# The last product's result turned to rows by VectorE in squares of 32 and by transfers in runs of 128 bytes, all but two regions

## The chip, the cores and the metric

One NeuronCore of a Trainium2 chip runs the whole kernel in one launch. The time is the device time of an execution in microseconds; beside it stands the span, which the profile measures from the first to the last instruction. In the text PE is TensorE, DVE VectorE, ACT ScalarE, POOL GpSimd and SP SyncE. SP and ACT each issue transfers on a queue of their own (q1 and q10 in the profile); both queues are served by the core's 16 DMA engines.

## The reference

A graph of 3327 nodes with 512 features each, all in float32, goes through two layers. Both use the same adjacency matrix.

```python
# layer 0
h = maximum(layernorm(x), 0)
q, k, v = h @ Wq.T + bq, h @ Wk.T + bk, h @ Wv.T + bv
x = x + softmax(q @ k.T / sqrt(512) + adj + adj) @ v
# layer 1
h = maximum(layernorm(x), 0)
A2 = adj + eye(3327)
dscale = diagonal(A2) ** (-0.5)
temp = A2 @ h @ W.T
x = x + relu((dscale[:, None] * A2 * dscale[None, :]) @ temp)
```

## The kernel before

The rows are padded to 26 tiles of 128 (`NT = 26`). After the scores of layer 0 come three large products of a 3328 x 3328 matrix with a matrix of 512 columns, numbered `g = 0, 1, 2`: the softmax weights times the normalised rows, A2 times the normalised rows of layer 1, and A2 times the scaled `temp`. All three run by a two-level recursion that needs seven products instead of eight at each level. The order of the seven outer products is `ORDER` (line 30: p5, p1, p6, p7, p2, p3, p4).

The columns of the left matrix, which are the rows of the result, lie in two strips `s` with two halves `y` each. A half of strip 0 is seven tiles wide (`H[0] = 896`), one of strip 1 six (`H[1] = 768`). For every outer product and strip there are seven steps: six with a pair of inner tiles, in which PE makes 14 matmuls (seven inner products, two for the strip's operands), and one with the odd tile (`None`) with eight. This gives 3 x 7 x 2 x 7 = 294 steps, which `run(k)` records one by one (line 1238). The steps of the last three outer products of `g = 2` are 252 to 293.

The result is held turned: `cts[s][y][d]` is a tile with 128 of the 512 features on the partitions (`d` is the block of features) and the 896 or 768 rows of that half along the free dimension. PE accumulates in eight PSUM banks; DVE and ACT gather them into these tiles at the end of each outer product (`Gather.first`, `rest` and `settle`, lines 948 to 981), and ACT puts earlier parts into the banks beforehand (`seed`, line 940). A region, that is a half `y` and a pair of feature blocks (`z = d // 2`), is complete at different times: both strips of (y=1, z=1) after p7, (0, 0) after p2, (0, 1) after p3, (1, 0) after p4, the last product.

Step `k` records, in this order: the load of step `k + 3`'s left operands on SP (`Step.load`, lines 820 to 827), the loads that are due (`between` tasks with "load" in their name), the matmuls of step `k`, the stores that became due (`deliver`, line 787: a store is issued on ACT's queue in a later step than the one that made its data), DVE's sums of operands for step `k + 2` (lines 163 to 165), and the other tasks that are due. The order of every engine's instructions is fixed as recorded (`in_order`, line 111). The built program hands eight completion semaphores for transfers around in turn, for SP's and ACT's transfers together: each issue waits until the eighth transfer before it has landed.

The last matter of the kernel is `finish` (line 1112). For each of the 26 row tiles PE turns four 128 x 128 blocks of `cts` into a PSUM bank (`turned`, line 1098, matmul with the identity, line 1102), ACT applies the relu with the factor `sd` of each row while reading the bank (line 1118), DVE adds the row tile of layer 0's result, which `finish_load` (line 1086) brought from `x1d` in DRAM (line 1119), and ACT's queue stores 128 rows to `out` (line 1120). Twenty of the tiles are done whole, one or two in a step, between steps 274 and 291, some of them in the middle of a step's matmuls (`within`). Tiles 20 to 25 (strip 1, y = 1) are done in two halves: the features of z = 1 in steps 254 to 259, those of z = 0 after the last step, by `turn_last` and `finish` from six different banks. `sd` is made at step 6 from the diagonal of the adjacency matrix, loaded in single elements (`prepare`, line 732; `prepared`, line 734).

`by_32` (line 147) holds 104 columns, one for each 32 rows. Before, it serves for the row sums of the softmax alone: DVE turns the sums in squares of 32 (line 596), and `place_totals` at step 3 reads the tile by a matmul (line 666).

## Time and profile before

| | us |
|---|---|
| median of 3 runs | 2166.16 |
| lowest and highest run | 2164.62, 2168.46 |
| the profiled execution | 2166.74 |
| its span | 2164.9 |

The profiled execution took 1.8 us more than its span. Busy shares by fortieths of the span, in tenths (9 is 90% or more), and the DMA queues of the whole run (packets, MB, share of the 16 engines' time):

```profile
PE   9999999999999999999999999999999999999998
PEld 5555555555555555555454555555666655555555
DVE  7479888888888688767777778886666567777676
ACT  5312211112110000001111000010111100001011
POOL 2000000000000000000111000000000000000000
PEclk9999999999999999999999999999999999999999
DMA  8678888888988899889797889886646368766695
...
q1 hardware_dynamic: 263096, 514.97, 70.2%
q10 hardware_dynamic: 35424, 69.62, 8.8%
```

A fortieth is 54 us. The steps 252 to 293 lie in the last four of them, from 1951.4 to 2153.0 us after the span's start. q1 is SP's queue, q10 ACT's. In the windows view each line gives a stretch in us from the span's start, its length, the busy time and number of instructions of PE, PEld (weight loads), DVE, ACT and POOL, the clock that PE was granted, the share of the DMA engines and GB/s.

### The profile page before, as it was taken

To read this page: it belongs to the slowest core of one execution; us is meant where nothing else is said; L and a number is where in the kernel's file an instruction comes from. 1 tells how busy PE (TensorE), PEld (TensorE's weight loads), DVE (VectorE), ACT (ScalarE), POOL (GpSimd) and SP (SyncE) were. 2 spreads that over 40 slices of the span, in tenths; PEclk is the share of its full clock that TensorE was granted. 3 is DMA by queue.
4 is the path that set the end of the run, shared out by engine and by line. 5 is a ranking of instruction groups with operands and counts; after the bars stand their busy time and mean duration, and the time that the engine had idled before them with its cause. 6 is when DMAs were issued, how large, how long until landed. Compare 5 with 4: busy or idle time off the path is not lost.

```text
span 2164.9 us, 21057 instructions
## 1 busy us (share of the span) xinstructions
PE 2148.5 (99%) x6364; PEld 1189.5 (55%) x6364; DVE 1627.2 (75%) x3218; ACT 289.6 (13%) x467; POOL 51.1 (2%) x62
## 2 busy tenths in 40 slices
PE   9999999999999999999999999999999999999998
PEld 5555555555555555555454555555666655555555
DVE  7479888888888688767777778886666567777676
ACT  5312211112110000001111000010111100001011
POOL 2000000000000000000111000000000000000000
PEclk9999999999999999999999999999999999999999
DMA  8678888888988899889797889886646368766695
GB/s 299 214 256 301 295 311 280 305 294 299 334 302 301 292 365 335 279 291 311 264 314 258 301 296 373 300 301 217 207 133 225 129 193 294 245 191 211 211 312 191
DMA packets 298643, 586.02 MB, mean 271 GB/s; under 512 B 31244, under 2 KB 166296, under 8 KB 298520
## 3 DMA queue, kind: packets, MB, share of 16 engines
q1 hardware_dynamic: 263096, 514.97, 70.2%
q10 hardware_dynamic: 35424, 69.62, 8.8%
q8 instruction: 53, 0.87, 0.2%
q14 instruction: 70, 0.57, 0.1%
HBM read 416.63 MB, written 167.84 MB: 270 GB/s over the span
## 4 chain that ended last, share of the span: by engine, by line
PE 92%; DVE 4%; DMA 3%; issue 1%; POOL 0%; ACT 0%; SPq 0%; DVEq 0%; ACTq 0%
PE p L909 54%; PE Y L541 13%; PE Z L541 6%; PE p L900 5%; PE p L1012 4%; PE pw L1073 3%; PE X L541 3%; PE Y L397 2%; DMA rows<-row 1%; PE Z L397 1%; DMA part<-p 1%; PE pt L1102 1%; PE X L397 0%; DVE part L163 0%; DMA wk<-in_wk_dram 0%
## 5 line engine op out<-in xcount | busy, mean ns | idle before, releaser
L909 PE MATMUL p<-part,b 128*128 128x448 f32 (+1 forms) x3528 | 1262.3, 513 | 1.0 <-DVE part L164 0.5
L909 PEld LDWEIGHTS p<-part,b 128*128 128x128 f32 x3528 | 667.6, 190 | 536.1 <-issue 287.7
L163 DVE TENSOR_TENSOR part<-part 128x896 f32<-128x896 f32 (+1 forms) x252 | 256.9, 1019 | 69.8 <-DMA part<-sum 27.9
L541 PE MATMUL Y<-qt,hp 128*128 128x448 f32 (+1 forms) x832 | 308.2, 513 | 1.0 <-DVE g L545 0.6
L541 PEld LDWEIGHTS Y<-qt,hp 128*128 128x128 f32 x832 | 157.7, 190 | 134.7 <-issue 72.7
L541 PE MATMUL Z<-qt,hp 128*128 128x384 f32 (+1 forms) x416 | 162.3, 512 | 0.0
L165 DVE TENSOR_TENSOR part<-part,part 128x448 f32<-128x448 f32 (+1 forms) x219 | 129.5, 591 | 15.3 <-PE p L909 0.5
L164 DVE TENSOR_TENSOR part<-part,part 128x448 f32<-128x448 f32 (+1 forms) x219 | 129.4, 591 | 7.2
L900 PE MATMUL p<-part,b 128*128 128x448 f32 (+1 forms) x336 | 124.2, 513 | 0.0
L541 PEld LDWEIGHTS Z<-qt,hp 128*128 128x128 f32 x416 | 79.0, 190 | 66.2 <-issue 37.9
L545 DVE SCALAR_TENSOR_TENSOR g<-g,Y 128x384 f32<-128x384 f32 (+1 forms) x156 | 91.4, 586 | 29.9 <-PE Y L541 28.8
L900 PEld LDWEIGHTS p<-part,b 128*128 128x128 f32 x336 | 63.7, 190 | 53.5 <-issue 31.4
L952 ACT COPY part<-p 128x384 f32<-128x384 f32 (+1 forms) x33 | 16.6, 502 | 551.2 <-PE p L909 428.4
L548 ACT ACTIVATE g<-g 128x768 f32<-128x768 f32 (+1 forms) x48 | 43.0, 896 | 345.3 <-DVE g L545 303.0
L541 PE MATMUL X<-qt,hp 128*128 128x384 f32 (+1 forms) x208 | 81.1, 512 | 0.0
L953 DVE TENSOR_TENSOR part<-p,part 128x384 f32<-128x384 f32 (+1 forms) x33 | 19.3, 585 | 68.1 <-PE p L909 65.0
L1012 PE MATMUL p<-w,ct 128*128 128x512 f32 x136 | 61.6, 592 | 0.0
L541 PEld LDWEIGHTS X<-qt,hp 128*128 128x128 f32 x208 | 39.5, 190 | 33.1 <-issue 19.3
L972 DVE TENSOR_TENSOR ct<-p,part 128x448 f32<-128x448 f32 (+1 forms) x72 | 43.0, 611 | 19.4 <-PE p L900 14.4
L1073 PE MATMUL pw<-w,rows 128*128 128x256 f32 x208 | 53.5, 380 | 0.4 <-DVE rows L1063 0.4
L1003 DVE TENSOR_TENSOR job<-job 128x896 f32<-128x896 f32 (+1 forms) x52 | 52.9, 1018 | 0.1
L190 POOL TENSOR_TENSOR rstd<-ve,mhalf 128x1 f32<-128x1 f32 x46 | 38.3, 835 | 556.5 <-DVE ve L188 520.8
(191 smaller groups left out, 1679.7 us busy)
## 6 DMA issues: line engine op xcount, KB each, us to landing
part<-sum SPq DMA_DIRECT2D x104, 448.0 KB, 4.9
part<-p SPq DMA_DIRECT2D x91, 448.0 KB, 5.8
part<-sum SPq DMA_DIRECT2D x104, 384.0 KB, 3.6
part<-p SPq DMA_DIRECT2D x91, 384.0 KB, 4.1
part<-in_adjT_dram SPq DMA_DIRECT2D x78, 448.0 KB, 5.0
b<-row SPq DMA_DIRECT2D x234, 128.0 KB, 4.7
part<-in_adjT_dram SPq DMA_DIRECT2D x78, 384.0 KB, 3.7
g<-in_adjT_dram SPq DMA_DIRECT2D x52, 448.0 KB, 4.1
```

What stands on the lines that cost most here:

```text
L163: yield nc.vector.tensor_add(o[:, 0:2], g[:, 0:4:3], g[:, 1:2].to_broadcast([P, 2, g.shape[-1]]))
L164: yield nc.vector.tensor_add(o[:, 2], o[:, 1], g[:, 0])
L165: yield nc.vector.tensor_add(o[:, 3], o[:, 2], g[:, 2])
L397: nc.tensor.matmul(ps[:, :w], M[B[name]][:, c, o * P : (o + 1) * P], hp[k][:, A[name], c], start=start and c == 0, stop=c == 1, skip_group ...
L541: nc.tensor.matmul(ps[:, :wd], h_of(self.t, name, k), qt[B[name]][:, k], start=start and k == 0, stop=k == 1, skip_group_check=True)
L545: nc.vector.scalar_tensor_tensor(a[n], a[n], 2.0, ps[:, :wd], op0=ALU.mult, op1=ALU.add if sign > 0 else ALU.subtract)
L548: nc.scalar.activation(g[1], g[1], AF.Exp, **({"bias": pad} if self.t == HALF - 1 else {}))
L900: yield nc.tensor.matmul(ps[("p2", "p3", "p4", "p8")[k]][:, :w], b[:, z], a[:, 0, y], start=k == 3 and not self.seeded, stop=True, skip_gr ...
L909: yield nc.tensor.matmul(ps[r][:, :w], b[:, i], m, start=self.t == 0 and not adds, stop=self.t == PAIRS - 1 and r in ("p1", "p5", "p6", "p ...
L1003: nc.vector.tensor_add(self.a, self.a, self.b)
L1012: nc.tensor.matmul(ps, cts[s][y][d][:, k * P : (k + 1) * P], w[d], start=d == 0, stop=d == DC - 1)
L1073: nc.tensor.matmul(ps, a, W[B[name]][:, c], start=new and c == 0, stop=c == 1, skip_group_check=True)
```

## The change

The unit of the turning is no longer a row tile but a column block `Columns(s, y, d)`: the whole tile `cts[s][y][d]`, 128 features by 896 or 768 rows. Of the 16 blocks 14 are turned without PE, eight of strip 0 and six of strip 1. What is left to the old way are the last two, d = 0 and 1 of strip 1, y = 1, that is the first half of the features of row tiles 20 to 25, after the last step.

A column block is loaded, turned, scaled and added in four tasks:

- `load`, two steps ahead: the matching part of layer 0's result is read from DRAM by four transfers on ACT's queue, one for each 32 partitions. Partition 32a + r of the tile receives, for each j, the 32 numbers of row 32j + r at features 128d + 32a onward, a run of 128 bytes; a transfer has 32 x 28 or 32 x 24 such runs.
- `turn`: one DVE instruction turns all squares of 32 x 32 of the tile. Partition 32a + r then holds the same runs, of the result, as the loaded tile does.
- `scale`, one step later: relu and the factor of each row in one DVE instruction. The factors come from `by_32`, which now also holds `(diagonal + 1) ** -0.5`, in each group of 32 partitions anew; each is read 32 times in a row.
- `add`, one more step later: DVE adds the loaded tile, and four stores in runs of 128 bytes are posted to ACT's queue.

The blocks begin at step 252 and follow each other every three steps, the last two steps after the one before. Two tiles take turns for the loaded part and two for the turned one. For the factors, four transfers on SP's queue at step 5 load the diagonal into `by_32`, once for each 32 partitions, 3,328 single elements each; at step 11 DVE adds one and POOL takes the power. `x1d` becomes one DRAM tensor for each strip and half instead of one for each row tile. `sd` stays for the tiles of the old way and for `temp`.

```diff
-    x1d = [dram.tile([P, D], F32, name=f"x1d{i}") for i in range(NT)]
+    x1d = [[dram.tile([HT[s] * P, D], F32, name=f"x1d{s}{y}") for y in range(2)] for s in range(2)]
...
+    def load_diagonal():
+        with nc.allow_non_contiguous_dma(reason="the diagonal, once"):
+            for a in range(4):
+                nc.sync.dma_start(by_32[32 * a : 32 * a + 32], bass.AP(tensor=adjT.tensor, offset=adjT.offset,
+                                                                      ap=[[LD + 1, 32], [32 * (LD + 1), 4 * NT]]))
+
+    def scales():
+        nc.vector.tensor_scalar(by_32, by_32, 1.0, None, op0=ALU.add)
+        nc.gpsimd.tensor_tensor(by_32, by_32, mhalf.to_broadcast(by_32.shape), op=ALU.pow)
...
+    xp_slots = itertools.cycle([lambda k=k: view(2, 1)[:, 2 * k : 2 * k + 2].rearrange("p a w -> p (a w)") for k in range(2)])
+    turn_ring = ring(*spare[:2])
...
-    def finish_load(i, z=(0, 1)):
-        c0, c1 = z[0] * E, (z[-1] + 1) * E
-        xrs[i] = next(xr_slots)()
-        nc.scalar.dma_start(xrs[i][:, c0:c1], x1d[i][:, c0:c1])
...
+    class Columns:
+
+
+        def __init__(self, s, y, d):
+            self.s, self.y, self.d = s, y, d
+
+        def parts(self, tile, rows):
+
+            rows = rows.rearrange("(j r) (c a e) -> c a r j e", r=32, a=4, e=32)
+            return [(tile[32 * a : 32 * a + 32].rearrange("r (j e) -> r j e", e=32), rows[self.d, a]) for a in range(4)]
+
+        def load(self):
+            self.x = next(xp_slots)()[:, : H[self.s]]
+            for to, rows in self.parts(self.x, x1d[self.s][self.y]):
+                nc.scalar.dma_start(to, rows)
+
+        def turn(self):
+            self.o = turn_ring([P, H[0]], "turned")[:, : H[self.s]]
+            nc.vector.transpose(self.o, cts[self.s][self.y][self.d])
+
+        def scale(self):
+            j = (STRIPS[self.s] + self.y * HT[self.s]) * 4
+            o = self.o.rearrange("p (j e) -> p j e", e=32)
+            by = by_32[:, j : j + 4 * HT[self.s]].unsqueeze(2).to_broadcast(o.shape)
+            nc.vector.scalar_tensor_tensor(o, o, 0.0, by, op0=ALU.max, op1=ALU.mult)
+
+        def add(self):
+            nc.vector.tensor_add(self.o, self.o, self.x)
+            r0 = (STRIPS[self.s] + self.y * HT[self.s]) * P
+            for of, rows in self.parts(self.o, out[r0 : r0 + H[self.s]]):
+                post(rows, of)
...
-    within = {}
-    for (n, s, t), its in {
-        (5, 1, 1): (0,), (5, 1, 2): (1,), (5, 1, 3): (2,), (5, 1, 4): (3,), (5, 1, 5): (4,),
-        (6, 0, 1): (5,), (6, 0, 2): (6, 14), (6, 0, 3): (15, 16), (6, 0, 4): (17, 18),
-        (6, 1, 1): (19, 7), (6, 1, 2): (8, 9), (6, 1, 3): (10, 11), (6, 1, 4): (12, 13),
-    }.items():
...
-    for t, i in enumerate(range(20, NT)):
-        rows(2, number_of(2, 4, 0, t + 2), i, (1,))
+    k = number_of(2, 4, 0, 0)
+    for n, (s, y, d) in enumerate(((0, 1, 2), (0, 1, 3), (1, 1, 2), (1, 1, 3), (0, 0, 0), (0, 0, 1), (1, 0, 0),
+                                   (1, 0, 1), (0, 0, 2), (0, 0, 3), (1, 0, 2), (1, 0, 3), (0, 1, 0), (0, 1, 1))):
+        part = Columns(s, y, d)
+        for what, later in ((part.load, -2), (part.turn, 0), (part.scale, 1), (part.add, 2)):
+            at(k + later, what)
+        k += 3 if n < 12 else 2
...
-    for k, what in ((1, totals), (3, place_totals), (2, prepare), (6, prepared), (8, judge), (9, judged)):
+    for k, what in ((1, totals), (3, place_totals), (2, prepare), (6, prepared), (5, load_diagonal), (11, scales), (8, judge), (9, judged)):
```

## The prediction

> **What bounds the kernel now.** First the page's busy table and the chain of waits. The chain runs through TensorE (PE) for 92% of the span, PE is busy for 99% of it at the full granted clock; so the time is the sum of PE's instructions, as long as their operands are there in time.
>
> ```profile
> PE 2148.5 (99%) x6364; PEld 1189.5 (55%) x6364; DVE 1627.2 (75%) x3218; ACT 289.6 (13%) x467; POOL 51.1 (2%) x62
> ...
> PE 92%; DVE 4%; DMA 3%; issue 1%; POOL 0%; ACT 0%; SPq 0%; DVEq 0%; ACTq 0%
> ```
>
> Then the stretch that the change touches: the last three recursion products of the third matrix product, steps 252 to 293. In the windows view (busy us of PE, PEld, DVE, ACT, POOL, then clock, DMA share, GB/s) the last line is that stretch, the others its two heaviest parts.
>
> ```profile
> 2051.40:2083.50 32.10, 32.10 (x114) 19.59 (x113) 20.74 (x36) 5.15 (x9) 0.00 (x0) 1.00 0.91 313
> 2083.50:2122.10 38.60, 38.23 (x123) 20.31 (x122) 33.41 (x68) 7.37 (x12) 0.00 (x0) 1.00 0.87 294
> ...
> 1951.40:2153.00 201.60, 201.22 (x640) 112.55 (x639) 142.41 (x268) 29.05 (x51) 0.00 (x0) 1.00 0.72 240
> ```
>
> PE never waits there (0.4 us in 201.6), even where the DMA engines are 91% busy. VectorE (DVE) has 71% of the stretch, the DMA engines 72%. These two resources receive the new work.
>
> **What goes from PE.** Of 104 transposes 92 go: four for each of 20 row tiles, two for each of six. Their cost is the distance between the matmuls around them, in PE's timeline:
>
> ```profile
> 1967.43 0.38 PE L1102 MATMUL pt<-ident,part 128*128 128x128 f32 x2
> 1967.65 5.43 PE L909 MATMUL p<-part,b 128*128 128x448 f32 x14
> ...
> 2065.78 0.60 PE L1102 MATMUL pt<-ident,ct 128*128 128x128 f32 x4
> 2066.22 4.68 PE L909 MATMUL p<-part,b 128*128 128x384 f32 x14
> ```
>
> Four hold up the next matmul by 0.44 us (2065.78 to 2066.22), two by 0.22. 20 x 0.44 + 6 x 0.22 = 10.1 us, all on PE's path: the whole possible gain. The stretch would shrink to 191.5 us. ACT loses its 26 scalings by relu, which delayed nobody but the additions behind them.
>
> **What DVE gets.** 26 additions go (18.39 us for 32, less 2.25 for the six that stay: 16.1). For each of 14 column blocks come a transpose in squares of 32, a relu with scaling by a broadcast factor, and an addition, eight blocks 896 wide, six 768 wide.
>
> ```profile
> 2153.00:2165.00 12.00, 2.25 (x6) 0.78 0.22 72
> sum 213.60, DVE 18.39; mean DVE 2.63
> ...
> L596 DVE STREAM_TRANSPOSE acc<-acc x8: 567/604/639, 245.7 to 631.9; 128x384 f32<-128x384 f32 x4, 128x448 f32<-128x448 f32 x4
> ...
> L163 DVE TENSOR_TENSOR part<-part 128x896 f32<-128x896 f32 x126 | 136.9, 1087 | 47.9 <-DMA part<-sum 22.1 <-DMA part<-p 21.2 <-DMA part<-in_adjT_dram 2.1
> L163 DVE TENSOR_TENSOR part<-part 128x768 f32<-128x768 f32 x126 | 120.0, 952 | 22.0 <-PE p L909 10.2 <-DMA part<-sum 5.8 <-DMA part<-p 3.6
> ```
>
> A transpose of half the width takes up to 0.57 to 0.64 us, so twice that at most, 1.25 and 1.13. The addition is L163's 1.09 and 0.95. The scaling with a broadcast factor has no row; from below it costs the addition (same elements, two sources), from above twice that if the broadcast is slow; I take the addition. 8 x (1.25 + 1.09 + 1.09) + 6 x (1.13 + 0.95 + 0.95) = 45.6 us. DVE then has 142.4 - 16.1 + 45.6 = 171.9 of 191.5 us, 90%. In the tightest part (2083.5 to 2122.1) it has 33.4 - 5.3 = 28.1 us, plus seven new instructions of about 1.03 = 35.3, beside 35.1 of PE (38.6 less eight tiles). That is level; DVE makes its sums two steps ahead (some 10 us), and that lead hides it. If the lead is gone, each microsecond over is one for PE. I allow 1.5 us for this and for product ends; bounds 0 and 5.
>
> **What the DMA engines get.** Each column block is loaded and stored in runs of 32 numbers: 128 x 28 or 128 x 24 packets each way, 8 x 3584 + 6 x 3072 = 47,104, so 94,208 in all. They replace 5,120 packets of 2 KB and 1,536 of 1 KB. Single packets of the trace, by size:
>
> ```
> bytes      4   512  1024  1536  1792  2048  3072  3584
> count  31116    12 39808 49920 45312 42368 44928 44928
> median ns  9  27.5    46    65    74    84   121   140
> ```
>
> This is a straight line, 8 ns plus 0.0371 ns a byte, and the line gives 12.8 ns for 128 bytes. The nearest rows bound it: 9 ns (4 bytes, though mostly single completions; the 3,328 diagonal elements took the same) and 27.5 ns (512 bytes). I take 12.8, near the 4-byte row by size. At these medians the data packets of the stretch now need 122 us of all 16 engines (145 as measured, stretched by contention). The removed ones are 31, the new ones 94,208 x 12.8 / 16 = 75: 166 of 191.5 us, 87%. With 9 ns it is 144, with 27.5 ns 253. Above 17.1 ns the engines no longer get through. Now 91% passes without PE waiting.
>
> [...]
>
> **Queues and waits.** All 112 new transfers are issued from ACT's queue, where 52 stood (0.33 us of issue each: 20 us more on an engine that has over 160 free). All transfers of SP and ACT share eight completion semaphores in turn, so each issue waits for the eighth before it; the profile shows SP held by ACT's transfers:
>
> ```profile
> SPq L847 <- DMA out_dram<-r: 1.6, 3, 1.0
> ...
> SPq L827 <- DMA part<-x1d: 0.9, 1, 0.9
> ...
> q1 hardware_dynamic: 15400, 35.49, 53.6%
> q10 hardware_dynamic: 8352, 12.85, 18.0%
> ...
> dg<-in_adjT_dram SPq DMA_DIRECT2D x1, 13.0 KB, 7.4
> ```
>
> Issues rise from 162 in 201.6 us to some 222 in 191.5, 1.16 per us: eight semaphores then allow a mean landing of 6.9 us, and the stretch's loads and stores now land in 2.6 to 7.3. From 2051.4 to 2083.5 there are already 37 issues in 32.1 us, 1.15 per us, with no PE wait. Behind a blocked store on ACT stand the copy (L952) and the seeds (L946) at each product's end, and behind those DVE's gathering and PE's next banks. I put this at 0 in the forecast; price if the cover is gone below.
>
> **The early part.** Four loads of 3,328 elements bring the diagonal into place at step 5: at 9 ns 7.5 us of all engines, on SP's queue ahead of the next operands (the present load of 3,328 lands in 7.4 us). DVE gets one small addition, POOL a power over 104 columns, four times L737's 5.1 us, while POOL idles. Operands are loaded three steps (some 15 us) ahead, so 0; up to 7.5 if that lead were spent.
>
> **Sum.** The profiled execution took 2166.74 us (span 2164.9 plus 1.8), 0.6 above the median of the runs, 2166.16. 2166.7 - 10.1 + 1.5 = 2158.1; against the median 2157.6. I say 2158.
>
> **Rivals.**
> 1. *The DMA engines become the bound* (slower). A 128-byte packet, above all one written to HBM, costs more than the line says. From 17.1 ns each further ns is 94,208 / 16 = 5.9 us. At 20 ns: 208 of 191.5, so 17 more, 2166.7 - 10.1 + 17 = 2174; at 27.5 ns 61 more, 2218. For it: no row of such stores, 5,900 runs per engine. Against: the straight line from 4 to 3584 bytes. 0.31.
> 2. *ACT's queue becomes the wait.* Column loads stand between PE's bank copies and seeds, waiting for semaphores that slow transfers hold. At six product ends, one landing of 4 to 5 us late, half of it hidden: 6 x 2 = 12 us; 2169, between 2163 and 2175. Against: the same issue rate now costs nothing. 0.13.
> 3. *DVE becomes the bound*: the broadcast scaling at twice the price adds 14 us, 186 of 191.5 with local excess of some 8: 2166, between 2161 and 2172. Against: scaling by a per-partition factor costs what an addition does. 0.09.
> That the transposes stay on PE is ruled out: the built program has 92 fewer.
>
> **How the numbers follow.** Forecast case 0.47, its own range 2154 to 2162. This kernel's measurement tells 0.2%, 4.3 us, from no change. The second rival falls half in no change and half in slower, the third two thirds and one third: faster 0.47, same 0.12, slower 0.41. The range begins at 2154 (the whole 10.1 without allowance, less the runs' spread of 2 us) and reaches to 2195, the first rival at 23.7 ns; beyond lies about a third of that rival, 0.1, and what falls under 2154 or beside the cases, 0.06.
>
> **What would show it.** Right: PE has 92 transposes fewer and still no idle time over 1 us in the stretch; 128-byte packets take near 13 ns; DMA share about 0.9; DVE 0.9. Wrong: PE waits for DVE's sums, and those for operand loads that land after 10 us or more (first rival); copies and seeds on ACT that wait for transfers (second); DVE without gaps while PE waits (third).

## The result, and the profile after

| | us |
|---|---|
| before, median of 6 runs | 2166.74 (2164.62 to 2168.46) |
| after, median of 6 runs | 2186.91 (2185.22 to 2189.25) |
| ratio | 1.0094, 95% interval 1.0081 to 1.0107 |
| the profiled execution after, and its span | 2186.69, 2184.8 |

The change makes the kernel slower, by 20.2 us. The span grows by 19.9 us, so the trace holds the whole loss. In the changed kernel 9 is added to the old line numbers of the matmuls and of the gathering: L909 is now L918 (L900 for the odd step is L909), the seeds are L955, ACT's bank copy L961. New are the column loads (L1141), turns (L1145), scalings (L1151), additions (L1154) and, through the common `post`, the column stores (L795).

The page of the changed kernel, busy table and chain of waits, as before:

```profile
PE 2145.7 (98%) x6272; PEld 1183.8 (54%) x6272; DVE 1653.1 (76%) x3235; ACT 273.0 (12%) x441; POOL 69.1 (3%) x63
...
PE 90%; DMA 4%; DVE 3%; ACTq 1%; issue 1%; ACT 0%; SPq 0%; POOL 0%; DVEq 0%
```

92 instructions and 2.8 us of busy time are gone from PE, and yet it carries 90% of the chain instead of 92%: transfers now end what is followed back. Where PE stands still is seen in its timeline (start, length, count, and in brackets the idle time before it and what ended it), lines of the last stretch:

```profile
1951.60 31.73 PE L918 MATMUL p<-part,b 128*128 128x448 f32 x84
...
2022.67 1.65 PE L909 MATMUL p<-part,b 128*128 128x384 f32 x2 [7.01 <-ACT p L955]
2024.11 33.33 PE L918 MATMUL p<-part,b 128*128 128x448 f32 x84
...
2097.35 1.65 PE L909 MATMUL p<-part,b 128*128 128x384 f32 x2 [7.40 <-ACT p L955]
2098.79 4.22 PE L918 MATMUL p<-part,b 128*128 128x448 f32 x6
2109.19 31.28 PE L918 MATMUL p<-part,b 128*128 128x448 f32 x78 [6.18 <-ACT p L955]
...
2173.22 2.16 PE L1110 MATMUL pt<-ident,part 128*128 128x128 f32 x12
```

The first and the last of these groups in the kernel before:

```profile
1951.65 15.95 PE L909 MATMUL p<-part,b 128*128 128x448 f32 x42
...
2155.14 1.58 PE L1102 MATMUL pt<-ident,part 128*128 128x128 f32 x12
```

Three times PE waits for ACT to put a seed into a bank, at the ends of two products' seven steps of strip 1: once before two matmuls of the odd step of p2, and in p3 there and again a step later. With one short wait of 0.20 that is 20.8 us. ACT's timeline around the first of them says what ACT was doing. `ACTq` lines are transfers being issued; their length is from the first issue of the group to the end of the last:

```profile
2004.84 9.54 ACTq L1141 DMA_DIRECT2D part<-x1d  x4
2016.30 5.28 ACTq L795 DMA_DIRECT2D out_dram<-turned  x4
2021.62 0.48 ACT L961 COPY part<-p 128x384 f32<-128x384 f32 x1 [32.54 <-DMA out_dram<-turned]
2022.13 0.49 ACT L955 ACTIVATE p<-ct 128x384 f32<-128x384 f32 x1
```

Eight issues take from 2004.8 to 2021.6 us, where eight of the old ones needed 8 x 0.34 us (the row stores' line of the kernel before: shortest, median and longest issue in ns):

```profile
L1120 ACTq DMA_DIRECT2D out_dram<-r x26: 338/344/446, 1969.6 to 2149.7; - x26
```

The copy stands behind them in the program, the seed behind the copy, and PE's next two matmuls behind the seed. The copy starts when the last store of a column block has been issued, not when its own bank is ready.

The idle time is not all. In the windows view the granted clock (the third number from the end) after two of the stalls, and well after the first:

```profile
2022.60:2026.10 3.50, 3.43 (x5) 1.85 (x6) 3.33 (x9) 0.02 (x1) 0.00 (x0) 0.50 1.04 145
...
2029.60:2060.30 30.70, 30.70 (x84) 15.46 (x83) 23.41 (x43) 1.08 (x2) 0.00 (x0) 1.00 0.83 202
...
2097.30:2100.80 3.50, 3.45 (x5) 1.85 (x6) 3.29 (x10) 0.00 (x0) 0.00 (x0) 0.50 0.27 38
```

PE comes back at half its clock, 0.50 in both windows. Now the account nearly closes: PE's last transposes start at 2155.1 us before and at 2173.2 after, 18.1 later. Idle time gives +20.4 (20.8, less 0.4 that PE waited before), the transposes that went -10.1, and the lower clock 6.8, which the last section works out from the lines above; 1.0 us of the 18.1 stays open. From there to the end of the span the tail grew from 9.8 to 11.6 us; ACT's last relus also wait for column stores, 8.8 us. 18.1 + 1.8 = 19.9.

What was not it: step 252 began on PE at 1951.60 us after and at 1951.65 before, so no cost of the work in the early part is seen. (In the kernels below with the same early part it began between 1948.8 and 1955.7 us, so a cost of a few us would not show.) And the short packets have the price that was forecast: 87,040 of them between 1951 and 2170 us took 13 ns (median; mean 13.8).

### The profile page after: what moved, and what is told of

Read it like the earlier page. It is cut to its first block, busy times and chain, and to the rows that moved or that the text cites. A ratio compares the mean times of both kernels' runs of the same rounds, so it can differ in the third digit from the quotient of the medians.

```text
span 2184.8 us, 20926 instructions
## 1 busy us (share of the span) xinstructions
PE 2145.7 (98%) x6272; PEld 1183.8 (54%) x6272; DVE 1653.1 (76%) x3235; ACT 273.0 (12%) x441; POOL 69.1 (3%) x63
## 4 chain that ended last, share of the span: by engine, by line
PE 90%; DMA 4%; DVE 3%; ACTq 1%; issue 1%; ACT 0%; SPq 0%; POOL 0%; DVEq 0%
PE p L918 52%; PE Y L541 13%; PE Z L541 7%; PE p L909 4%; PE p L1025 4%; PE pw L1086 3%; PE X L541 3%; PE Y L397 2%; PE Z L397 1%; DMA part<-sum 1%; DMA part<-x1d 1%; DMA part<-in_adjT_dram 1%; ACTq L795 1%; DMA rows<-row 0%; PE X L397 0%
## 5 line engine op out<-in xcount | busy, mean ns | idle before, releaser
L918 PE MATMUL p<-part,b 128*128 128x448 f32 (+1 forms) x3528 | 1263.7, 514 | 7.5 <-ACT p L955 7.0
L918 PEld LDWEIGHTS p<-part,b 128*128 128x128 f32 x3528 | 672.1, 191 | 553.8 <-issue 296.8
L909 PE MATMUL p<-part,b 128*128 128x448 f32 (+1 forms) x336 | 126.2, 518 | 14.4 <-ACT p L955 14.4
L909 PEld LDWEIGHTS p<-part,b 128*128 128x128 f32 x336 | 64.1, 191 | 69.2 <-issue 31.7
L961 ACT COPY part<-p 128x384 f32<-128x384 f32 (+1 forms) x33 | 16.6, 502 | 678.9 <-PE p L918 384.1
```

The costliest lines, as they stand in the source:

```text
L909: yield nc.tensor.matmul(ps[("p2", "p3", "p4", "p8")[k]][:, :w], b[:, z], a[:, 0, y], start=k == 3 and not self.seeded, stop=True, skip_gr ...
L918: yield nc.tensor.matmul(ps[r][:, :w], b[:, i], m, start=self.t == 0 and not adds, stop=self.t == PAIRS - 1 and r in ("p1", "p5", "p6", "p ...
```

## The experiments

Theory Q puts the loss down to ACT's queue: transfers that wait there for completion semaphores hold up copies and seeds. Theory D puts it down to the time and place that the short packets take on the DMA engines. All times are medians, each compared with the kernel before on the same chip (medians of 2166.2 to 2167.7 us); "waits" is PE's idle time over 0.1 us between step 252 and the last transposes, from each kernel's timeline; "landing" is the median time from issue to landing of the column loads and stores between 1985 and 2140 us. Waits and landings belong to the one profiled execution, which can lie some us from the median (e1 2158.4, e7 2175.2, e10 2183.7 us).

| kernel | us | ratio to before (95%) | waits, us | landing, us |
|---|---|---|---|---|
| changed | 2186.9 | 1.0081 to 1.0107 | 20.8 | 5.5, 4.9 |
| e1: columns issued by POOL | 2162.3 | 0.9969 to 0.9988 | 0 | 7.5, 5.5 |
| e2: long runs on ACT | 2163.3 | 0.9971 to 0.9996 | 4.1 | stores 3.7 |
| e3: no column transfers | 2155.2 | 0.9939 to 0.9973 | 0 | - |
| e4: columns issued by SP | 2182.0 | 1.0052 to 1.0085 | 12.5 | - |
| e5: behind copies and seeds | 2186.3 | 1.0067 to 1.0110 | 21.2 | - |
| e6: POOL but for last stores | 2160.3 | 0.9956 to 0.9978 | 1.5 | - |
| e7: loads by POOL | 2178.1 | 1.0033 to 1.0071 | 13.8 | stores 7.7 |
| e8: stores by POOL | 2169.4 | 0.9999 to 1.0018 | 6.8 | loads 5.8 |
| e9: right operands by POOL | 2187.4 | 1.0074 to 1.0105 | 23.4 | 5.3, 4.3 |
| e10: long loads | 2178.9 | 1.0039 to 1.0070 | 14.8 | - |
| e11: long stores | 2173.9 | 1.0025 to 1.0055 | 11.8 | - |
| e12: x1 written turned | 2158.7 | 0.9955 to 0.9979 | 0 | - |
| e13: copies and seeds on DVE | 2185.7 | 1.0063 to 1.0100 | 19.9 | - |
| e14: light operands | 2170.0 | 1.0004 to 1.0023 | 9.1 | 3.6, 3.1 |
| e15: left operands by POOL | 2180.5 | 1.0042 to 1.0075 | 15.2 | 4.8, 4.9 |
| e16: light, and by POOL | 2165.9 | 0.9981 to 1.0000 | 5.2 | 3.7, 3.1 |

**Queue or packets: four extremes.** The first changes the issuing queue alone:

```diff
             for to, rows in self.parts(self.x, x1d[self.s][self.y]):
-                nc.scalar.dma_start(to, rows)
+                nc.gpsimd.dma_start(to, rows)
...
             for of, rows in self.parts(self.o, out[r0 : r0 + H[self.s]]):
-                post(rows, of)
+                posted.append((now[0], lambda of=of, rows=rows: nc.gpsimd.dma_start(rows, of)))
```

> The changed kernel with the column blocks' loads and stores issued by POOL instead of ACT; packets and bytes are the same. Theory Q (ACT's in-order queue: the bank copy and the seeds stand behind column transfers that wait for completion semaphores): PE's 20.8 us of waits for ACT's seeds in the last stretch go, and with them the slower clock after them; about 2157 to 2163 us. Theory D (the DMA engines' time for 128-byte packets is what makes everything late): the engines have the same work, so still 2178 us or more.

The second keeps ACT's queue and the number of transfers, and makes every run as long as a partition of the tile:

```diff
-            for to, rows in self.parts(self.x, x1d[self.s][self.y]):
-                nc.scalar.dma_start(to, rows)
+            for a in range(4):
+                nc.scalar.dma_start(self.x[32 * a : 32 * a + 32], self.flat(x1d[self.s][self.y], a))
```

and the stores likewise.

> As many column transfers on ACT's queue, with the same bytes, but each partition's part in one run of 3584 or 3072 bytes instead of 28 or 24 runs of 128; the numbers land in other places of the result than the reference has them. Theory Q: the number of transfers and the semaphores that they hold are the same, so most of the loss stays, 2175 us or more, and PE still waits for ACT's seeds. Theory D: the 75 us of DMA time for 128-byte packets becomes about 55, the engines are no longer crowded, and the time falls to 2157 to 2163 us.

The third takes the column transfers out; the addition reads the tile that is not turned:

```diff
-            nc.vector.tensor_add(self.o, self.o, self.x)
+            nc.vector.tensor_add(self.o, self.o, cts[self.s][self.y][self.d])
```

> The column blocks are turned, scaled and added on DVE as in the changed kernel, but nothing of them is loaded or stored: the addition takes the unturned tile as its second operand, and 14 of the 16 blocks of the result are not written. Theories Q and D both expect 2156 to 2159 us (the time before less the 10.1 us of transposes, plus little). If DVE's added work is the bound (a third theory), PE waits for DVE's sums and the time stays above 2163 us.

The fourth is the first with `nc.sync` in the place of `nc.gpsimd`.

> The column blocks' loads and stores issued by SP instead of ACT, on the queue of the operand loads. Theory Q in its narrow form (what matters is what stands behind the column transfers on ACT): ACT's copies and seeds are on time, 2157 to 2165 us. If the shared completion semaphores alone are at fault, operands become late instead, PE waits for DVE's sums, and the time is 2170 us or more. Theory D: 2178 us or more.

Either change by itself, another queue (2162.3) or longer runs (2163.3), takes back some 24 us. So neither the queue nor the packets cost alone; the loss needs both. (By the packet prices of the prediction the long runs need 30 us of all engines, not the 55 of the expectation.) Without column transfers the kernel takes 2155.2 us. From the start of step 252 to PE's last transposes it is 193.0 us there (1952.25 to 2145.21) against 203.5 before (1951.65 to 2155.14): 10.5 us less, the 10.1 of the forecast and the 0.4 that PE waited before. The windows view of this kernel:

```profile
1951.40:2150.00 198.60, 195.72 (x568) 106.45 (x566) 172.03 (x296) 15.23 (x32) 0.00 (x0) 1.00 0.57 187
```

DVE is busy for 172.0 us there, and PE never waits for it: DVE is not the bound. On SP's queue the column transfers hold up the operand loads instead (DVE's sums wait 41 us for them); PE then waits mostly for DVE's gathering, 9.3 of 12.5 us, and little is won. On POOL's queue they land later than on ACT's (7.5 and 5.5 us), and PE does not wait: nothing that it needs stands behind them there, and in the built program POOL's transfers count on eight semaphores of their own. So a late landing by itself cost nothing here; nor did the load of the engines as a whole, whose share from 1951.4 to 2150 us is 0.89 here and 0.90 in the changed kernel. POOL's queue shows 3,584 packets of 2 to 4 KB beside completions, where 94,208 runs of 128 bytes are moved: many runs go into one packet. So this experiment changes the packets too, and does not say which of the two helped.

**Is it the order in ACT's queue?** The same transfers on the same queue, but those that are due in the last two steps of a half are recorded behind that half's copy and seeds:

```diff
+        held = 252 <= k < len(steps) - 1 and t in (PAIRS - 1, None)
...
-        deliver(k)
+        if not held:
+            deliver(k)
         if t is None:
...
+        if held and t is None:
+            deliver(k)
+            while later:
+                later.pop(0)()
```

> The changed kernel with the same transfers, in the same runs of 128 bytes, on the same queue (ACT's). Only their place in ACT's program changes: those column loads and stores that the changed kernel issues in the last two steps of a half are issued behind that half's copy and seeds instead of ahead of them. Theory Q (transfers that wait for a completion semaphore hold up the copy and the seeds behind them in ACT's queue): PE's three waits for ACT's seeds, 20.8 us together, go or shrink under 5 us in all, and the time falls by 18 us or more, to 2157 to 2168 us. Theory D (the engines' time for 94,208 short packets is what costs, wherever they stand): 2180 us or more, with waits of PE that now end at DVE's sums or at operand loads. A mixed result of 2168 to 2180 would say that the queue carries some of it and late operand loads the rest.

2186.3 us: nothing won, against the expectation of theory Q; theory D missed as well, as PE's three waits still end at ACT's seeds. ACT's timeline of this kernel:

```profile
1997.05 9.41 ACTq L1141 DMA_DIRECT2D part<-x1d  x4
2007.64 7.62 ACTq L795 DMA_DIRECT2D out_dram<-turned  x4
2015.56 5.42 ACTq L1141 DMA_DIRECT2D part<-x1d  x4
2021.03 0.48 ACT L961 COPY part<-p 128x384 f32<-128x384 f32 x1 [33.32 <-DMA part<-x1d]
```

The copy now has four column transfers fewer ahead of it (32 instead of 36 since the first), and is as late: those that remain have become late in their turn. We read this as ACT running behind by a whole block, so that what stands last in the line does not matter.

**Moving a part to POOL.** Three kernels, each the first one with one thing less: the stores of the last two blocks back on ACT; only the loads on POOL; only the stores on POOL.

> All column transfers issued by POOL as in the first experiment, but for the stores of the last two column blocks, which go back to ACT's queue. In the first experiment PE ended its work 10.7 us earlier than in the kernel before, and the span only 8.4 us earlier: 12.0 us lay between the start of PE's last group and the end, against 9.8 before. If the last stores issued by POOL make this tail (they land later than others and share the engines with the last row stores), the tail falls to 9 to 10.5 us and the time to 2157 to 2160.5 us. If the tail has another cause (contention, whichever queue issues them), the time stays at 2161 to 2164 us; and if the ACT queue's eight stores hold up ACT's last relus as in the changed kernel (8.8 us of wait there), it rises to 2164 us or more.

> Half of the move: the column loads are issued by POOL, the column stores stay on ACT's queue. Theory Q: the copy and the seeds of two of the three stalls stand behind a store and a load in turn; with the loads gone 56 of the 112 transfers still stand in ACT's queue, but the issues that share eight semaphores fall from some 222 to some 166 in the stretch, as many as before the change, so each is had sooner: PE's waits fall from 20.8 to 0 to 6 us and the time to 2160 to 2170 us. Theory D (packets): 2180 to 2190 us, as many short packets run.

> The other half: the column stores are issued by POOL, the column loads stay on ACT's queue. Theory Q: as with the loads moved, 0 to 8 us of PE's waits stay, 2160 to 2172 us; if it is the stores alone that matter (the waits of the copy are put down to a column store each time), this kernel does as well as the one that moves both, 2158 to 2163 us, and the one that moves the loads does worse. Theory D: 2180 to 2190 us; a weaker form of it, that short writes to HBM are what costs, would leave this one at 2180 us or more as well, since the number of short writes is the same.

With the last stores back on ACT the time is 2160.3, and the interval overlaps that of the first kernel. The time is the one expected, but not for the reason expected: the tail after the start of PE's last group is 11.6 us (2147.90 to 2159.5) and not 9 to 10.5. Why this tail is longer than without column transfers (8.7) stays open. Halves give halves: 13.8 us of waits stay with the stores on ACT, 6.8 with the loads. The stores weigh more than the loads, but neither is all of it. For the loads alone both theories missed: 2178.1 us lies above the 2170 of theory Q and below the 2180 of theory D.

**Half of the short packets.** The long runs of the second experiment for the loads alone, then for the stores alone.

> The same 112 transfers on ACT's queue and the same bytes, but the loads in long runs (3.5 and 3 KB), the stores in runs of 128 bytes: half of the short packets. The loaded block is not the one that belongs there, so the sums of 14 blocks are of other numbers. With all short: 2186.9 us and 20.8 us of waits; with none: 2163.3 us and 4.1 us. If each short packet counts alike (the engines' load), this lies half way, 2172 to 2178 us. If short writes to HBM are what lasts, it stays at 2180 to 2187 us; if short reads are, it falls to 2163 to 2170 us.

> The mirror image: the stores in long runs, the loads in runs of 128 bytes; the result of 14 blocks is written to other places. If each short packet counts alike, 2172 to 2178 us; if short writes to HBM are what lasts, 2163 to 2170 us; if short reads are, 2180 to 2187 us.

2178.9 and 2173.9 us: 8.0 and 13.0 of the 23.6 us that both together bring (2186.9 to 2163.3). Short reads and short writes both count; that the writes count more is not clear of the noise, as the two intervals overlap. That short writes to HBM alone are what lasts is ruled out.

**The shared semaphores.** The right operands of the last three products leave SP's queue for POOL's:

```diff
-                nc.sync.dma_start(dst[:, k], src if z is None else src[:, z * E : (z + 1) * E])
+                queue = nc.gpsimd if self.g == 2 and self.r in ("p2", "p3", "p4") else nc.sync
+                queue.dma_start(dst[:, k], src if z is None else src[:, z * E : (z + 1) * E])
```

> The column transfers stay as in the changed kernel: 112 of them, in runs of 128 bytes, on ACT's queue. Instead SyncE is relieved: the right operands' rows of the last three products (p2, p3, p4 of the third matrix product) are loaded by POOL's queue, which has its own semaphores, so about a quarter of the issues that share eight semaphores leave the ring in the stretch, while the DMA engines move the same bytes in the same packets. If what holds ACT back is the common ring of semaphores, in which an ACT transfer waits for one of SyncE's that itself waits for PE, PE's 20.8 us of waits fall to 0 to 8 us and the time to 2160 to 2172 us. If the short packets themselves hold up ACT (each transfer simply takes too long), PE's waits stay at 15 us or more and the time at 2179 us or more.

2187.4 us and 23.4 us of waits: no gain. The mere number of issues that share the semaphores is not what counts.

**Is ACT's queue the link at all?** All transfers stay, and DVE makes the copies and seeds of the last three products:

```diff
-                        nc.scalar.mul(ps[k][:, : self.width], c, sign)
+                        if now[0] >= 252:
+                            nc.vector.tensor_scalar(ps[k][:, : self.width], c, float(sign), None, op0=ALU.mult)
+                        else:
+                            nc.scalar.mul(ps[k][:, : self.width], c, sign)
...
+            if behind:
+                nc.vector.tensor_copy(c11, p["p1"])
+                behind()
```

> The changed kernel with every transfer left as it is (112 column transfers in runs of 128 bytes, on ACT's queue, in the same places). Only the copies and the seeds of the last three recursion products (5 copies and 21 seeds, about 0.5 us each) are made by VectorE instead of ACT, so that no computing that PE waits for stands in ACT's queue behind a transfer. If ACT's in-order queue is the link (theory Q), PE no longer waits for ACT, DVE gains some 13 us of work (185 of some 191 us, so waits of 1 to 3 us for DVE at the ends of halves are to be expected), and the time falls from 2186.9 to 2160 to 2172 us. If the slow transfers reach PE in another way (late operands, late sums, late column blocks that stop DVE), PE's waits stay above 12 us in all, now put down to DVE or to a transfer, and the time stays at 2177 us or more.

2185.7 us, 19.9 us of waits: theory Q as it stood, with ACT's order as the only link, falls. Nothing that PE needs stands behind a transfer on ACT here, and PE waits as long, now for DVE. DVE's timeline tells why:

```profile
2051.60 0.98 DVE L1152 STREAM_TRANSPOSE turned<-ct 128x768 f32<-128x768 f32 x1 [8.46 <-DMA out_dram<-turned]
2083.09 0.96 DVE L1161 TENSOR_TENSOR turned<-turned,part 128x768 f32<-128x768 f32 x1 [9.48 <-DMA part<-x1d]
2091.07 1.11 DVE L1152 STREAM_TRANSPOSE turned<-ct 128x896 f32<-128x896 f32 x1 [4.90 <-DMA out_dram<-turned]
```

Within some 40 us a turn waits 8.5 us for the store that frees its tile, an addition 9.5 us for its load. The column transfers themselves get through too slowly: with two tiles for the loaded part and two for the turned one, a block's loads and stores are not done when the next but one needs the tile. In all DVE waits 37.5 us for column transfers here, and it carries ACT's copies and seeds besides, so the like size of the loss says little. In the changed kernel DVE never waits for them: ACT pays for that lateness and hands it on through its own program (DVE waits 34 us for ACT's copies there); here DVE does. More than two tiles of each kind were not tried. So the question becomes why the transfers are slow.

**Why slow: the company.** The queues view of the changed kernel in two windows of 3 us, first 2014 to 2017, where SP's transfers run too, then 2022 to 2025, where they don't (packets, MB, share of the engines' time, and one load issued in the first window with its time to landing):

```profile
q1 hardware_dynamic: 270, 0.75, 89.1%
q10 hardware_dynamic: 799, 0.10, 21.7%
...
part<-x1d ACTq DMA_DIRECT2D x1, 112.0 KB, 7.2
```

```profile
q10 hardware_dynamic: 3204, 0.40, 85.9%
```

Alone, 1,068 short packets a us pass: 85.9% of 16 engines, 13 ns each. Beside SP's packets of 1 to 3.5 KB it is 266, though a load that was issued at 2014.0 us is under way through the whole window and lands 7.2 us after its issue. Most of the 799 pass at once: 551 in the first half microsecond, and between 2015 and 2017 us only 115, beside 198 of SP's. At these rates the 896 packets of a transfer need 0.8 us in the one case and 3.4 in the other. The price of a packet is the same, a median of 13 ns in both windows; fewer of them get through: beside long packets the queue of short ones got 0.10 MB of 0.85. In what order the engines serve the two queues was not shown; both shares of the first window add up to 111%, so the engines had no time left in it.

The next kernel cuts the company: SP loads the left operands of the last three products for 32 partitions only, in the same packets.

```diff
-            nc.sync.dma_start(a[:, k], adjT[r0 : r0 + P, c0 : c0 + H[s]])
+            nc.sync.dma_start(a[:some, k], adjT[r0 : r0 + some, c0 : c0 + H[s]])
```

> The changed kernel, but the left operands of the last three recursion products are loaded for 32 of 128 partitions only (same packets, a quarter as many; the other 96 partitions keep what stood there, so these products are of other numbers). The number of transfers, their order, the queues and semaphores, and all 94,208 packets of 128 bytes stay. If competition with long packets is what makes the column transfers late, they land in 2 to 4 us, no issue of ACT lasts over 1 us, PE's waits fall from 20.8 us to 0 to 4 us and the time to 2155 to 2164 us. If ACT's queue itself, or the eight semaphores by the number of issues, is what is too slow, the waits stay above 12 us and the time at 2176 us or more.

2170.0 us: between the two expectations, 16.9 us of the 31.7 that lie between the changed kernel and the one without column transfers. The stores' line and their time to landing, from the view by source line; changed kernel first (shortest, median and longest issue in ns, the landing in us):

```profile
L795 ACTq DMA_DIRECT2D out_dram<-turned x40: 322/518/3755, 1984.8 to 2135.1; - x40
...
DMA to landing us min/median/max: 2.0/4.9/7.5
```

```profile
L795 ACTq DMA_DIRECT2D out_dram<-turned x43: 322/539/1008, 1985.5 to 2139.9; - x43
...
DMA to landing us min/median/max: 2.0/3.1/5.1
```

With less company a store lands in 3.1 us instead of 4.9, and no store's issue lasts over 1.0 us, where one lasted 3.8. (The longest issue of a load is 1.9 us, above the 1 us expected, and 2.7 in the changed kernel.) That is a second way in which ACT is held: not only the wait for a semaphore, but the issue of a transfer of many short packets itself becomes long when those before it have not drained; the last section has the counts. With long runs (e2) the longest issue of a store is 0.59 us.

**And the left operands' semaphores.** In what is left in that kernel, the fourth load of a block waits 4.8 us, until 2011.80, for a semaphore. By the order in which the eight are handed around, a left-operand load of SP's holds it, and for 2.7 us of the 4.8 that load has not been issued, as it waits for a matmul to free its tile. POOL takes these loads; with all operand bytes, and with a quarter of them:

```diff
+        queue = nc.gpsimd if late else nc.sync
...
-                nc.sync.dma_start(a[:, k], sumd[s][j][:, SUMS.index(what), :])
+                queue.dma_start(a[:, k], sumd[s][j][:, SUMS.index(what), :])
```

> The changed kernel, but the left operands of the last three recursion products (the loads that wait for PE to free their buffer) are issued by POOL, whose transfers don't take the eight semaphores that SyncE and ACT share. Bytes, short packets, and all of ACT's queue stay. If the waits for semaphores held by such loads are the smaller part and the competition of packets the larger, PE's waits fall from 20.8 to some 8 to 14 us and the time to 2168 to 2180 us. If the shared semaphores are the whole cause after all, to 0 to 3 us and 2155 to 2164 us; if they are nothing, the time stays at 2182 us or more.

> Both at once: the left operands of the last three products issued by POOL, and loaded for 32 of 128 partitions only (these products are of other numbers). If competition and the semaphores held by PE-bound loads are together the whole cause, PE has no wait over 1.5 us left and the time is 2155 to 2162 us, as without any column transfer (2155.2). If 2165 us or more, ACT's queue has a limit of its own for transfers of 768 and 896 packets.

| us (waits of PE) | left operands on SP | on POOL |
|---|---|---|
| all operand bytes | 2186.9 (20.8) | 2180.5 (15.2) |
| a quarter of them | 2170.0 (9.1) | 2165.9 (5.2) |

The two causes add up: the company of long packets 15 to 17 us, the left operands' place among the shared semaphores 4 to 6 us (with all bytes the time is just above the 2180 us that was expected at most). Of the last kernel's expectation the first case, no wait left, was missed: 10.7 us to the 2155.2 without column transfers stay, 5.2 of them waits for ACT. Its other case, 2165 us or more and a limit of ACT's queue of its own, is met by a hair. The 10.7 us can come from the short transfers' own crowd on ACT's queue, or from the right operands and the quarter of the left ones that still run beside them; this was not taken further apart.

**ACT's queue, counted.** In the changed kernel's trace, between 1985 and 2140 us, ACT stands 55 us until the transfer that holds the semaphore of its next issue has landed (4 us in the kernel before), and its 77 issues take another 55 us (16 us for 41 before). Of the 55 us at semaphores, 27 are held by column transfers, 20 by left operands and 7 by right ones, which fits that moving the right ones won nothing; and in only 4 of the 20 had the left operand not yet been issued, so it is mostly the landing that ACT waits for, and less the load's own wait for PE. Both sums together go with PE's waits in the nine kernels that have loads and stores on ACT's queue and its copies too: 85 to 90 us where PE waits 4 to 5 us (e16, e2), 94 to 100 where it waits 9 to 15 (e11, e14, e15), 106 to 128 where it waits 15 to 23 (e5, e9, e10 and the changed kernel).

**A better version.** If x1 is already turned when it is written, in the first matrix product, each column block is loaded by one transfer of long runs. The 104 stores of x1 that this needs, and the column stores, are issued by POOL; what the old way still reads of x1 is stored in rows besides. Nothing of the computation is left out.

```diff
-        post(x1_of(i), xt)
+        s, y, k = where(i)
+        for n in range(4):
+            to = x1t[s][y].rearrange("d (a r) (j e) -> j r (d a) e", r=32, e=32)[4 * k + n]
+            of = xt[32 * n : 32 * n + 32].rearrange("r (c e) -> r c e", e=32)
+            posted.append((now[0], lambda to=to, of=of: nc.gpsimd.dma_start(to, of)))
...
-            for to, rows in self.parts(self.x, x1d[self.s][self.y]):
-                nc.scalar.dma_start(to, rows)
+            nc.scalar.dma_start(self.x, x1t[self.s][self.y][self.d])
```

> A version meant to be better: x1 is written already turned, in the first matrix product (each row tile by four transfers in runs of 128 bytes, issued by POOL), so that a column block is loaded in one transfer of long runs on ACT's queue (14 instead of 56), and the column stores are issued by POOL. All of the computation is done. If ACT's queue and the eight semaphores are what costs, the last stretch has no wait of PE over 1 us, as with both on POOL, and with half as many short packets there its transfers land sooner: 2156 to 2161 us, against 2162.3 with all column transfers on POOL and 2155.2 without any. If the 104 stores of x1 hurt the first matrix product (POOL's queue or short packets there), some of it is given back there: 2162 to 2170 us, with the stretch before step 168 longer than in the kernel before.

2158.7 us in six runs (2157.2 to 2159.6), 0.33% faster than before (interval 0.21% to 0.45%), and as fast as the forecast for the change itself. PE has no wait in the last stretch. The window that was shown for the kernel without column transfers:

```profile
1951.40:2150.00 198.60, 193.43 (x561) 105.23 (x559) 170.21 (x293) 13.88 (x29) 40.77 (x56) 0.99 0.76 242
```

The clock is at 0.99, the DMA share at 0.76 instead of 0.90 in the same window, and the first product gives nothing back: step 252 begins at 1949.95 us, 1.7 earlier than before, which is within the spread given above. From there to PE's last transposes it is 193.0 us, as without column transfers; the tail behind them is longer, 12.6 us instead of 9.8.

## Why the prediction failed, point by point

**PE: right.** 92 transposes are worth 10.1 us; the kernel without column transfers needs 10.5 us less for PE's stretch, and 0.4 of that is a wait that PE had before. That this was the whole possible gain on PE holds too: 2155.2 is 11.5 below the kernel before, of which 1.1 lies in the tail (8.7 us instead of 9.8), and no version came lower.

**DVE: right.** The new instructions take 0.95 to 1.11 us each, and the scaling by a broadcast factor, which had no row, costs the same as an addition (0.95 us for 768 columns and 1.08 for 896, both of them, in the changed kernel). Over the forecast's stretch, 191.7 us from 1951.4 on, the kernel without column transfers has 166.3 us of DVE's work where 171.9 were forecast: the sum was somewhat high, as a turn took 1.10 or 0.97 us and not 1.25 or 1.13. (The 172.0 above belong to a window 6.9 us longer.) The allowance of 1.5 us was not needed. The third rival did not occur in the changed kernel.

**The packets' price: right, and it decided nothing.** 13 ns against 12.8, a DMA share of 0.88 against 87%. The first rival, as put (from 17.1 ns the engines no longer get through), did not occur. At 27.5 ns, the row for 512 bytes, it would have been some 2218 us; 13 ns, stores to HBM included, are on the line instead. What the sum left out is that 87% is a mean over the stretch: from 2014 to 2017 us the shares add up to 111%, and the mean says nothing of how soon the shorter packets get through. That the engines get through and a queue doesn't was in none of the cases.

**The early part: right** as far as it can be seen: 0 was forecast, and step 252 begins 0.05 us earlier than before, where kernels with the same early part differ by some us.

**Queues and waits: wrong, and this is the step that failed**: "Behind a blocked store on ACT stand the copy (L952) and the seeds (L946) at each product's end, and behind those DVE's gathering and PE's next banks. I put this at 0 in the forecast". The link was seen and priced at nothing, for two reasons that both fell. One was a mean: 1.16 issues per us, so eight semaphores "allow a mean landing of 6.9 us". The measured landings, 4.9 and 5.5 us, are below that, and PE waited 20.8 us. The semaphores go round in order and each issue waits for one certain transfer: ACT stood 55 us at semaphores between 1985 and 2140 us, where the forecast put nothing. The other was a precedent: the same rate, 1.15 per us, passed before without a wait. But then the transfers were of 1 KB and more; it was taken for granted that short runs at the same rate of issue would land in the same 2.6 to 7.3 us and be issued in 0.33 us each. The landings stayed near that range (2.0 to 7.5 us, though the stores' median rose from 3.0 for rows to 4.9); the issues did not, with 0.5 us in the median and up to 3.8, 55 us in all where 77 at 0.33 are 25.

**The second rival** names the place where PE stops: "Column loads stand between PE's bank copies and seeds, waiting for semaphores that slow transfers hold". It was put at 0.13 and at 12 us. In the trace two of six ends are hit, by 7.0 and 13.6 us and not by 2 each, and the clock adds 6.8 us and the tail 1.8 that the rival had no term for. It is also not the whole cause: with copies and seeds off ACT (e13) the loss stays, and with the transfers behind them (e5) as well. The first rival had the resource, the second the place; the mechanism joins them.

## What to carry to other kernels

Price a transfer in short runs by who else has packets on the engines, not by its packets alone: here a queue with packets of 128 bytes beside one with packets of 1 to 3.5 KB got 266 packets a us where it got 1,068 alone, while the engines' sum over the stretch still fitted. Then ask what stands in program order behind its issue, and who frees the semaphores it waits for; computing that another engine awaits does not belong on a queue that issues such transfers (PE waited 20.8 us with the column transfers on ACT's queue, and not at all with them on POOL's, where the packets were longer too). A wait of 6 to 7 us on PE cost 1.8 to 2.6 us more, because the clock fell to 0.50.

## What the runs showed of the hardware

The granted clock fell to half when PE waited for 7.01, 7.40 and 6.18 us. The rows above show it for the first two: 0.50 for the first 3.5 us after the stall at 2022.6 and for the first 3.5 us after the one at 2097.3, and 1.00 from 2029.6 on; behind the third it was 0.51 from 2109.2 to 2112.7. The 84 matmuls behind the first stall took 33.33 us instead of 31.73, and the two ahead of them 1.44 (from start to start) instead of 0.65, a quarter of the 2.58 that eight take: 2.4 us. Behind the second stall it is 0.8 us for two and 1.8 for the next six (4.22 us; in the kernel before, six take 2.42), behind the third 1.8 for 78: 6.8 us in all. By the trace's clock records the half clock lasted 6.8, 10.2 and 6.8 us, the end of each stall included. Beyond their own length the stalls cost 2.4, 2.6 and 1.8 us.

An issue on ACT's queue was not always 0.3 us: with 768 or 896 packets it took 0.52 us in the median of the changed kernel's stores, and up to 3.8 us. It went with the number of earlier short packets on the queue that have not started: with fewer than 600 of them an issue took 0.31 to 0.39 us (23 issues), with over 2,200 a median of 1.7 us (11 issues).

Transfers in runs of 128 bytes were not equal on all queues. Issued by POOL (e1) the same runs showed as packets of 2 to 4 KB (3,584 for 94,208 runs), at 0.72 to 0.75 us an issue.
